# Making the second tile of weights between the second and third bank of products, with the first tile taken by two engines and the statistics taken late

## The chip, the cores and the metric

One core of a Trainium2 chip. The metric is the time of one execution on the device, in microseconds (us). The 23 runs of the kernel before on one chip lie within 0.3% of their median (4170.98 to 4191.01 us, median 4181.48). The kernel before takes 4181 us (median of 4 runs, 4176.17 to 4183.92).

## The reference, cut to what matters

Two layers. Each normalises x by groups, makes a convolution's weights for every batch element and position from a small network of z, multiplies, and adds the result to x. All is fp32.

```python
h = jax.nn.relu(_ln(z @ W1 + b1, g1, be1))
w = (h @ W2 + b2).reshape(B, L, CI, CO, K)      # weights of its own for each (b, l)
...
x_uf = jnp.stack([xp[..., i:i + L] for i in range(K)], axis=-1)
out = jnp.einsum('sbilk,bliok->sbol', x_uf, w)
out = out + bias[None]
# layer n: x = x + conv(_gn(x), ...), S2 = B = 32, CI = CO = 64, L = 256, K = 3
```

## The kernel before

The main loop runs over half batch elements `v` (64 per layer, 128 in all); one turn is called a period here. In each period TensorE makes 12 tiles of the next weights, k0 to k11 (`make`, 32 pairs of load and matmul each, 4 KiB of PSUM per partition, as much as two banks of products), and multiplies the present weights with x (`products`, four banks of PSUM, 80 pairs each). VectorE and ScalarE move the tiles into `wall`, the present weights (`take`); VectorE adds a bank of products to x (`room`) and takes the statistics for the next layer (`bn_stats`, layer 0 only). A tile may be moved into `wall` only when all products of the weights there are done. There are three buffers for tiles and two for products.

```python
ps_g = ctx.enter_context(tc.tile_pool(name="ps_g", bufs=3, space=PSUM))   # tiles of weights
ps_c = ctx.enter_context(tc.tile_pool(name="ps_c", bufs=2, space=PSUM))   # banks of products
...
def make(h, kind, o0):
    pg = ps_g.tile([P, OG, M], FP, tag="pg", name="pg")
    ...
    for k in range(OG):
        nc.tensor.matmul(pg[0:C, k, :], ...)      # line 459
        nc.tensor.matmul(pg[C:P, k, :], ...)      # line 460

def take(pg, n, kind, o0, scalar=False):
    ...
    if kind < 2:                       # all 128 partitions by VectorE
        (add_scalar if scalar else add)(slice(0, P), CH + (1 + kind) * CH)
    else:                              # lower half VectorE, upper half 8 instructions of ScalarE
        (add_scalar if scalar else add)(slice(0, C), CH + F)
        add_scalar(slice(C, P), 0)

def products(v):
    for q in range(NB):                # NB = 4
        pc = ps_c.tile([P, EB, CH], FP, tag="pc", name="pc")
        ... 80 pairs, line 505
        nc.vector.tensor_tensor(part, pc..., part, ALU.add)          # line 515
        if u < B:
            for g in range(2 * q, 2 * q + 2):
                bn_stats(parts[:, g, u, h, :], y, g)                 # line 246

order = [(kind, o) for o in starts for kind in (2, 0, 1)]
...
for v in range(1, NH * U):
    for k in range(len(order)):
        weights(v, k, False, (lambda: products(v - 1)) if k == 0 else None)   # make k0, products, take k0
        if k == 0:
            after(v - 1)               # stores, loads, next normalisation
```

## Time and profile before

| | before |
|---|---|
| time, median of 4 | 4180.99 us |
| span of the profiled run | 4177.9 us |
| period in layer 0, mean of 59 | 30.74 us |
| period in layer 1, mean of 60 | 28.91 us |
| nothing but TensorE's work (12 tiles, 4 banks, 2 changes of tile size) | 28.3 us |

The last row is the smallest period of the trace. TensorE is the bound (94% busy, and 84% of the chain that ended last), so only what makes it stand counts. "Holes" are its standing inside the products for no recorded cause; "the wait before k3" is its standing for a PSUM buffer after the products. Times of one place in all periods (the holes by their place, a tile's 32 pairs) were read off the start times of TensorE's weight loads in the trace, counted from the first product of the period. The prediction's 30.88 stands beside 30.74 here: it is met as the mean of 62 periods with the second of the loop (33.1 us) and the first two at the border between the layers (39.0 and 28.9) in it, which the table leaves out. From here on I use the table's choice for every kernel alike.

### The profile page before, as it was taken

How to read it: one execution, taken by the hardware profiler on the slowest of the kernel's cores; microseconds unless marked ns; L12 is line 12 of the kernel's file. 1: busy time of each engine (PE TensorE's matmuls, PEld its weight loads, DVE VectorE, ACT ScalarE, POOL GpSimd, SP SyncE). 2: the span in 40 equal slices, each digit the busy share in tenths (PEclk: the TensorE clock that was granted, in tenths of full speed). 3: DMA queues.
4: the chain of work that ended last, by engine and by line, in shares of the span. 5: the costliest groups of instructions: out<-in, count | busy, mean ns of one | idle time of the engine just before them, and what ended most of it. 6: DMA issues, size and time to landing. Idle time of an engine off the chain costs nothing.

```text
span 4177.9 us, 193861 instructions
## 1 busy us (share of the span) xinstructions
PE 3923.3 (94%) x90704; PEld 3746.7 (90%) x90704; DVE 2622.5 (63%) x2926; ACT 1325.8 (32%) x4384; POOL 2038.6 (49%) x628
## 2 busy tenths in 40 slices
PE   5777999999999999999998899999999999999999
PEld 3447999999999999899998899999999999999998
DVE  5686666666666666666666565655656556566565
ACT  3462322323323233232332333333323333333332
POOL 3435445445545544544551644555445554455542
PEclk8679999999999999999999999999999999999999
DMA  7875776767767677677776544544445444445442
GB/s 288 313 289 144 187 175 175 178 165 182 178 172 187 161 185 176 168 184 166 182 178 173 180 156 135 166 148 145 156 136 166 149 144 156 147 155 161 132 151 89
DMA packets 655581, 718.50 MB, mean 172 GB/s; under 512 B 568564, under 2 KB 585016, under 8 KB 586296
## 3 DMA queue, kind: packets, MB, share of 16 engines
q1 hardware_dynamic: 627796, 692.41, 58.5%
q8 instruction: 709, 11.62, 1.2%
q10 hardware_dynamic: 26980, 13.69, 1.1%
q14 instruction: 96, 0.79, 0.1%
HBM read 492.08 MB, written 213.91 MB: 169 GB/s over the span
## 4 chain that ended last, share of the span: by engine, by line
PE 84%; DVE 6%; issue 3%; DMA 2%; POOL 2%; ACT 1%; ACTq 0%; POOLq 0%; DVEq 0%; SPq 0%
PE pg L459 54%; PE pc L505 24%; PE pg L460 5%; DVE wall L471 3%; POOL xn L201 2%; DVE parts L246 1%; DVE room L515 1%; DMA hd<-xn 1%; ACT xn L218 1%; DMA zt<-in_L_conv_z_dram 1%; ACT xn L193 1%; POOL xn L446 1%; PE p L190 0%; DMA wc<-in_L_conv_Wb_dram 0%; DVE xn L446 0%
## 5 line engine op out<-in xcount | busy, mean ns | idle before, releaser
L459 PE MATMUL pg<-hT,w2t 128*64 128x128 f32 x24576 | 2733.6, 273 | 23.2 <-DVE wall L471 14.0
L460 PE MATMUL pg<-hT,w2t 128*64 128x128 f32 x24576 | 2734.3, 273 | 1.7 <-issue 1.6
L459 PEld LDWEIGHTS pg<-hT,w2t 128*64 128x64 f32 x24576 | 2683.3, 137 | 48.4 <-DVE wall L471 29.0
L460 PEld LDWEIGHTS pg<-hT,w2t 128*64 128x64 f32 x24576 | 2682.5, 137 | 3.4 <-issue 3.1
L471 DVE TENSOR_TENSOR wall<-pg,b 64x1024 f32<-64x1024 f32 x1527 | 1854.3, 1220 | 679.2 <-PE pg L460 675.2
L482 ACT ACTIVATE wall<-pg,b 64x128 f32<-64x128 f32 x4168 | 1203.8, 484 | 2662.4 <-DVE wall L471 2030.5
L436 POOL TENSOR_TENSOR xn<-room,gmean 128x2048 f32<-128x2048 f32 x124 | 581.8, 4692 | 1751.5 <-PE pc L505 1719.2
L505 PE MATMUL pc<-wall,xn 128*32 128x128 f32 (+2 forms) x40960 | 994.5, 253 | 133.3 <-issue 107.6
L505 PEld LDWEIGHTS pc<-wall,xn 128*32 128x32 f32 x40960 | 938.0, 111 | 196.7 <-issue 170.9
L515 DVE TENSOR_TENSOR room<-pc,room 128x512 f32<-128x512 f32 x512 | 354.3, 692 | 753.4 <-PE pc L505 676.6
L436 POOL TENSOR_TENSOR xn<-xn,rstd 128x2048 f32<-128x2048 f32 x124 | 746.8, 6022 | 9.7
L409 POOL TENSOR_TENSOR room<-room,bt 128x2048 f32<-128x2048 f32 x128 | 592.1, 4626 | 119.1 <-DMA bt<-bd 119.1
L246 DVE BATCH_NORM_STATS2 parts<-room 128x6 f32<-128x256 f32 (+1 forms) x592 | 241.6, 454 | 8.7
L201 POOL TENSOR_TENSOR xn<-xn 128x512 f32<-128x512 f32 (+2 forms) x192 | 104.1, 542 | 154.3 <-ACT xn L193 141.7
L190 PE MATMUL p<-wc,zt 17*128 17x256 f32 x256 | 88.4, 500 | 28.9 <-DMA zt<-in_L_conv_z_dram 28.9
L216 PEld LDWEIGHTS p<-ident,xn 128*128 128x128 f32 x256 | 50.0, 223 | 63.4 <-issue 63.4
L190 PEld LDWEIGHTS p<-wc,zt 17*128 17x128 f32 x256 | 60.8, 250 | 49.5 <-issue 27.9
L246 DVE BATCH_NORM_STATS2 parts<-wall 128x6 f32<-128x512 f32 x160 | 97.3, 677 | 7.8 <-DMA beb<-in_L_conv_beb_dram 7.8
L228 PE MATMUL p<-xn,Wb 128*64 128x512 f32 x64 | 55.2, 960 | 31.2 <-ACT xn L218 31.2
L216 PE MATMUL p<-ident,xn 128*128 128x128 f32 x256 | 61.9, 422 | 18.2 <-DVE xn L207 18.2
L205 DVE RECIPROCAL var<-var 128x8 f32<-128x8 f32 x32 | 6.4, 201 | 71.3 <-ACT var L202 71.3
L228 PEld LDWEIGHTS p<-xn,Wb 128*64 128x64 f32 x64 | 7.6, 169 | 47.2 <-ACT xn L218 44.6
(58 smaller groups left out, 266.7 us busy)
## 6 DMA issues: line engine op xcount, KB each, us to landing
bt<-bd SPq DMA_DIRECT2D x512, 256.0 KB, 5.9
room<-in_xp_dram SPq DMA_DIRECT2D x64, 1024.0 KB, 9.2
room<-in_xs_dram SPq DMA_DIRECT2D x64, 1024.0 KB, 8.2
x<-room SPq DMA_DIRECT2D x64, 1024.0 KB, 5.3
x1p<-room SPq DMA_DIRECT2D x512, 128.0 KB, 6.9
room<-x1p SPq DMA_DIRECT2D x64, 1024.0 KB, 7.9
room<-x SPq DMA_DIRECT2D x64, 1024.0 KB, 8.3
out_dram<-room SPq DMA_DIRECT2D x64, 1024.0 KB, 4.8
```

Of the source, the lines that this page charges most:

```text
L190: nc.tensor.matmul(self.p1[:, k], self.zt[:, k * P : (k + 1) * P], self.t["wc"], start=True, stop=True)
L201: nc.gpsimd.tensor_tensor(to, self.sq[:, :, 0:w], self.sq[:, :, w : 2 * w], ALU.add)
L216: nc.tensor.transpose(p2[:, net, k * P : (k + 1) * P], hs[:, 2 * k + net, :], ident)
L246: nc.vector.bn_stats(out, y.rearrange("p o (a m) -> p o a m", a=2)[:, :, :, g * e : (g + 1) * e])
L409: nc.gpsimd.tensor_tensor(y, y, bts.pop(v), ALU.add)
L436: nc.gpsimd.tensor_tensor(o, i, b, op)
L459: nc.tensor.matmul(pg[0:C, k, :], w[:, k0 * C : (k0 + 1) * C], h0, start=True, stop=True)
L460: nc.tensor.matmul(pg[C:P, k, :], w[:, k1 * C : (k1 + 1) * C], h1, start=True, stop=True)
L471: nc.vector.tensor_tensor(place(rows, a), pg[rows].rearrange("p o (t m) -> p t m o", t=NT), b2[n][rows, kind, None, None, o0 : o0 + OG].to ...
L482: nc.scalar.activation(place(rows, a)[:, :, :, k], pg[rows, k].rearrange("p (t m) -> p t m", t=NT), AF.Identity, bias=b2[n][rows, kind, o0 ...
L505: nc.tensor.matmul(pc[t * S : (t + 1) * S, n0 - q * EB : n1 - q * EB, :], xn[:, u % 2, t * MT + p + 1, :], wall[:, t, a : a + (n1 - n0) * CH],
L515: nc.vector.tensor_tensor(part, pc.rearrange("p (m a) o -> p o a m", a=2), part, ALU.add)
```

## The change

The intent: give TensorE a tile of weights to make amid the products, end the wait for the first tile sooner by sharing it between two engines, and keep the statistics out of the way of it. The core of the diff:

```diff
-        def take(pg, n, kind, o0, scalar=False):
+        def take(pg, n, kind, o0, scalar=0):
+            vector = OG - scalar          # columns 0..vector-1 VectorE, the rest ScalarE
...
-        order = [(kind, o) for o in starts for kind in (2, 0, 1)]
+        order = [(kind, o) for o in starts for kind in (0, 2, 1)]
...
-        products(NH * U - 1) and bn_stats inside products
+        products(v, banks), statistics(v, banks)
...
+        first, second = range(0, NB // 2), range(NB // 2, NB)
         for v in range(1, NH * U):
-            for k in range(len(order)):
-                weights(v, k, False, (lambda: products(v - 1)) if k == 0 else None)
-                if k == 0:
-                    after(v - 1)
+            pg0 = made(v, 0)
+            products(v - 1, first)
+            statistics(v - 1, first)
+            pg1 = made(v, 1)
+            products(v - 1, second)
+            taken(v, 0, pg0, OG // 2)     # k0: four columns VectorE, four ScalarE
+            statistics(v - 1, second)
+            after(v - 1)
+            taken(v, 1, pg1)
+            for k in range(2, len(order)):
+                weights(v, k)
```

(The two lines on `products` and `statistics` stand for a longer piece of the diff; nothing else is in it but names.)

More of the change, by code (lines that the diff above doesn't have):

```diff
@@ L468, in place, with add_vector @@
                 return at(wall[rows, 0, a : a + 1], [[WT, NT], [F, MT], [1, OG]])
-            def add(rows, a):
+            def add_vector(rows, a):
                 nc.vector.tensor_tensor(
-                    place(rows, a),
-                    pg[rows].rearrange("p o (t m) -> p t m o", t=NT),
-                    b2[n][rows, kind, None, None, o0 : o0 + OG].to_broadcast(
-                        [rows.stop - rows.start, NT, MT, OG]
+                    place(rows, a)[:, :, :, 0:vector],
+                    pg[rows, 0:vector].rearrange("p o (t m) -> p t m o", t=NT),
+                    b2[n][rows, kind, None, None, o0 : o0 + vector].to_broadcast(
+                        [rows.stop - rows.start, NT, MT, vector]
                     ),
@@ L478, in add, with add_scalar @@
                 )
-            def add_scalar(rows, a):
-                for k in range(OG):
+            def add_scalar(rows, a, k0):
+                for k in range(k0, OG):
                     nc.scalar.activation(
@@ L487, in add_scalar, with add, products @@
                     )
+            def add(rows, a):
+                if vector:
+                    add_vector(rows, a)
+                add_scalar(rows, a, vector)
             if kind < 2:
-                (add_scalar if scalar else add)(slice(0, P), CH + (1 + kind) * CH)
+                add(slice(0, P), CH + (1 + kind) * CH)
             else:
-                (add_scalar if scalar else add)(slice(0, C), CH + F)
-                add_scalar(slice(C, P), 0)
-        def products(v):
+                add(slice(0, C), CH + F)
+                add_scalar(slice(C, P), 0, 0)
+        def products(v, banks):
             u, h = divmod(v, NH)
             y = residual(v)
-            for q in range(NB):
+            for q in banks:
                 pc = ps_c.tile([P, EB, CH], FP, tag="pc", name="pc")
@@ L515, in products, with statistics @@
                 nc.vector.tensor_tensor(part, pc.rearrange("p (m a) o -> p o a m", a=2), part, ALU.add)
-                if u < B:
-                    for g in range(2 * q, 2 * q + 2):
-                        bn_stats(parts[:, g, u, h, :], y, g)
+        def statistics(v, banks):
+            u, h = divmod(v, NH)
+            if u < B:
+                for g in range(2 * banks.start, 2 * banks.stop):
+                    bn_stats(parts[:, g, u, h, :], residual(v), g)
         def next_pairs(w, k):
@@ L560, in conv_layers, with made, taken @@
         starts = range(0, CH, OG)
-        order = [(kind, o) for o in starts for kind in (2, 0, 1)]
-        def weights(v, k, scalar=False, between=None):
+        order = [(kind, o) for o in starts for kind in (0, 2, 1)]
+        def made(v, k):
+            u, h = divmod(v, NH)
+            kind, o = order[k]
+            return make(hs[u], kind, h * CH + o)
+        def taken(v, k, pg, scalar=0):
             u, h = divmod(v, NH)
@@ L567, in weights @@
             o0 = h * CH + o
-            pg = make(hs[u], kind, o0)
-            if between:
-                between()
             take(pg, n, kind, o0, scalar)
@@ L573, in weights @@
                 load_w2(n + 1, o0, o0 + OG)
+        def weights(v, k, scalar=0):
+            taken(v, k, made(v, k), scalar)
         def first_weights():
@@ L579, in first_weights @@
             for k in range(9):
-                weights(0, k, True)
+                weights(0, k, OG)
         first_phase(first_weights)
@@ L605, in conv_layers @@
                     next_pairs(B + 1, 0)
-        products(NH * U - 1)
+        products(NH * U - 1, range(NB))
         after(NH * U - 1)
```

## The prediction

> **What bounds the kernel now.** I read the page first: its busy table, its chain and its costliest groups. TensorE is the bound, and nearly all of the chain that ended last is its own work.
>
> ```profile
> PE 3923.3 (94%) x90704; PEld 3746.7 (90%) x90704; DVE 2622.5 (63%) x2926; ACT 1325.8 (32%) x4384; POOL 2038.6 (49%) x628
> PE 84%; DVE 6%; issue 3%; DMA 2%; POOL 2%; ACT 1%; ACTq 0%; POOLq 0%; DVEq 0%; SPq 0%
> L471 DVE TENSOR_TENSOR wall<-pg,b 64x1024 f32<-64x1024 f32 x1527 | 1854.3, 1220 | 679.2 <-PE pg L460 675.2
> L482 ACT ACTIVATE wall<-pg,b 64x128 f32<-64x128 f32 x4168 | 1203.8, 484 | 2662.4 <-DVE wall L471 2030.5
> q8 instruction: 709, 11.62, 1.2%
> ```
>
> The main loop runs 127 times ("periods"): 12 tiles of weights (k0 to k11, 32 load-and-matmul pairs each, 1.747 us a tile when nothing waits) and four banks of products (80 pairs each, about 1.765 us a bank). Layer 0 has 62 such periods away from the border between the layers, mean 30.88 us; layer 1 has as many, mean 28.91 us. The undisturbed sum is 12 x 1.747 + 4 x 1.765 = 28.02 us, plus 0.28 us for the two changes of tile size (from 64-column to 32-column weights 0.31 us pass between two loads, every time; back again 0.15 us). So layer 0 loses about 2.5 us a period and layer 1 about 0.6. Where, the chain of waits shows for one period of layer 0, in order of time (start, us, what):
>
> ```profile
> 2036.98 3.50 PE pc L505 x145
> 2040.49 0.82 issue
> 2041.31 2.88 PE pc L505 x113
> 2044.19 0.88 issue
> 2045.07 1.37 PE pc L505 x44
> 2046.44 0.02 issue
> 2046.46 0.70 DVE room L515
> 2047.16 0.02 issue
> 2047.19 0.75 DVE parts L246 x2
> 2047.94 2.26 DVE wall L471 x2
> 2050.20 0.04 issue
> 2050.24 0.32 PE pg L459
> ```
>
> Two things are lost here. First, two holes of "issue" inside the products. Second, after the products VectorE adds the last bank, takes two statistics and two tiles before TensorE gets a free PSUM buffer: TensorE makes k1 and k2 meanwhile and then stands 0.47 us before k3. (Mean of k3's slot in layer 0: 2.22 us, not 1.75; in layer 1, without statistics, 1.75.)
>
> The timeline of the weight loads says what the holes are:
>
> ```profile
> 2041.31 2.61 PEld L505 LDWEIGHTS pc<-wall,xn 128*32 128x32 f32 x128 [1.06 <-issue]
> 2045.07 1.19 PEld L505 LDWEIGHTS pc<-wall,xn 128*32 128x32 f32 x47 [1.15 <-issue]
> ```
>
> From hole to hole there are 128 loads and 128 matmuls, 256 instructions. In the whole trace the holes in the products sit at one place of every 256 TensorE instructions, and 181,536 of these over 256 is 709, the number of packets of the instruction queue above. TensorE runs dry of instructions: a block of products alone takes 128 x 0.022 = 2.8 us, and a new block comes 3.05 us (no hole before) to 3.6 us (after a hole) later[...]. A block with a tile of weights in it lasts 4 us and never waits. Means of the holes at the block borders (position counted in loads from the first product): layer 0, even periods 0.84 (80 to 95), 1.04 (208 to 223), 0.06 (336 to 351); odd 0.21 (16 to 31), 0.87 (144 to 158), 1.05 (272 to 286). Layer 1 even 0.01 (53 to 67), 0.26 (179 to 194), 0.64 (307 to 322); odd 0.02, 0.02 and 0.28 (243 to 259).
>
> [...]The trace has ScalarE starting only when VectorE's operation on the same tile has ended (the 2030.5 us above), although they read different halves of the partitions. In the changed tile k0 VectorE reads columns 0 to 3 and ScalarE 4 to 7, 2 KiB each[...]. [...]the trace has 1220 and 692. So VectorE's half of k0 is estimated at 0.69 us, 0.62 from its start to the next start, since the trace starts the next operation about 0.08 before the end.
>
> **The change part by part, per period.**
>
> (1) A tile (k1) goes between the second and third bank. Stream now: k0, 160 product pairs, k1 (32), 160 pairs, k2 to k11. Block borders keep their places. Layer 0 even: the border at 208 to 223 now ends a block that holds k1, so its 1.04 goes to 0; the one at 336 to 351 now ends a block of pure products: 2.8 us against some 3.15, so 0.06 becomes about 0.35; the first falls from 0.84 to about 0.40 because TensorE stands before the block's products anyway (part 3). Sum 1.94 to 0.75. Odd: 0.21 goes to 0 (same reason), 0.87 stays (a block of the first two banks only), 1.05 goes to 0. Sum 2.13 to 0.87. Mean -1.22 us. Layer 1 even: 0.91 to 0.25; odd 0.30 to 0.02; mean -0.47 us. One more change of tile size there and back: +0.28 us.
>
> (2) What VectorE does after the last bank. k0 and k1 now both sit in PSUM, so after the products TensorE has one free buffer (k2), then k0's (k3); k4 needs k2's (k1 is kind 2, its ScalarE part ends later still). VectorE's line, counted from k2's first load: add starts 0.16, next start 0.73 on, half of k0 0.62, four statistics 1.34 (twice the 0.67 that two take in the timeline), k1 1.12, k2 1.21 to its end, 0.05 to TensorE: 5.23 us. TensorE needs 1.69 + 1.75 = 3.44 for k2 and k3. So it stands 1.79 us before k4, in place of 0.47 before k3: +1.3 us in layer 0. In layer 1 without statistics the add-to-take step is 0.61: 0.16 + 0.61 + 0.62 + 1.12 + 1.21 + 0.05 = 3.77, a wait of 0.33 in place of 0. The late statistics do help k0 and k3, but k4 pays for them.
>
> (3) The order of kinds goes from (2,0,1) to (0,2,1). Kind 2 is the one whose eight ScalarE instructions start only after VectorE's, and it moves from k9 to k10, one tile nearer to the products, which read its zone from the first matmul on. In the period above:
>
> ```profile
> 2033.09 2.27 ACT L482 ACTIVATE wall<-pg,b 64x128 f32<-64x128 f32 x8 [2.97 <-DVE wall L471]
> 2064.05 2.47 ACT L482 ACTIVATE wall<-pg,b 64x128 f32<-64x128 f32 x8 [2.97 <-DVE wall L471]
> ```
>
> These end at 2035.36 and 2066.52; the products start at 2036.91 and 2067.86. One tile (1.747) later plus 0.05 for the semaphore, ScalarE ends at 2037.16 and 2068.31: the products wait 0.25 and 0.45 us. Over all periods the two values alternate, mean +0.355 us.
>
> Sum, layer 0: -1.22 + 0.28 + 1.3 + 0.355 = +0.72 us; layer 1: -0.47 + 0.28 + 0.33 + 0.355 = +0.50 us. Times 62 each: +44 and +31, in all +75 us, so 4257; I say 4255 (+1.8%). Busy work of VectorE and ScalarE hardly changes (127 halves of a tile to ScalarE, about 1.4 us each, beside other work). The phase before the loop and the border between the layers stay.
>
> **The rivals.** (a) The intended gain: the tile in the middle ends the fetch holes, and ScalarE's help with late statistics ends the wait before k3. If parts 2 and 3 cost nothing, the time falls by (1.22 - 0.28 + 0.47) x 62 + (0.47 - 0.28) x 62 = 99 us, to about 4085. Against it: the order of VectorE's queue and the three buffers are fixed by the program, and 5.23 against 3.44 is not close. (b) The fetch holes only move: the blocks find their wait at other borders, and part 1 gives 0.4 us less in each period. Then about 4305, slower by 3%. For it: [...]a block of pure products still exists in most periods. (c) All fetch holes vanish: at most 0.8 us more in layer 0 and 0.15 in layer 1, about 4198. (d) ScalarE's half of k0 is ordered after VectorE's all the same: k3 waits a microsecond more, hidden behind k4's wait in layer 0, but some 0.7 us in layer 1: about 4298. Against it: ScalarE's writes of kind 2 and VectorE's of the next tile interleave in the same zone without waiting (2048.98 and 2049.17 in the trace).
>
> **Range and chances.** The waits of parts 2 and 3 rest on durations that the trace repeats within a few hundredths; the fetch term is the loose one, by about 0.4 us a period either way, some 40 us. Range 4215 to 4300. The limit of 2% slower is 4265, ten above my figure, so: faster 0.04, within 2% 0.55, slower 0.41.
>
> **What would show it.** Right: the chain shows a VectorE wait of 1.6 to 1.9 us before the fifth tile (k4) in layer 0 and 0.2 to 0.5 in layer 1, with k0, four statistics, k1, k2 ahead of it; the first products wait for ScalarE (L482's successor) 0.25 and 0.45 in turn; "issue" holes in the products fall by about half, none left at borders whose block holds the middle tile. Wrong: no wait before k4 (part 2 falls, and the time is below 4180), or "issue" before products as large as now (part 1 falls, and it is above 4300).

## The result, and the profile after

The changed kernel takes 4291.07 us (median of 4 runs, 4282.81 to 4295.07), the one before 4180.99 us. The ratio is 1.0262 (95% interval 1.0243 to 1.0280): slower by 2.6%. Ratios here are the mean time of one kernel's runs over that of the other's of the same rounds, so not quite the ratio of the medians. The range held; the class I had given the most weight (within 2%, 0.55) did not come, the next one (0.41) did.

From the page of the changed kernel: the busy table, the chain, and groups of section 5.

```profile
PE 3972.5 (93%) x90704; PEld 3746.1 (87%) x90704; DVE 2509.8 (58%) x2926; ACT 1477.1 (34%) x4892; POOL 2037.0 (47%) x628
...
PE 71%; DVE 13%; ACT 9%; issue 3%; DMA 2%; POOL 2%; ACTq 0%; SPq 0%; POOLq 0%; DVEq 0%
...
L459 PEld LDWEIGHTS pg<-hT,w2t 128*64 128x64 f32 x24576 | 2675.9, 137 | 207.6 <-ACT wall L484 152.0
...
L484 ACT ACTIVATE wall<-pg,b 64x128 f32<-64x128 f32 (+1 forms) x4676 | 1354.6, 474 | 2621.2 <-DVE wall L473 2617.4
L473 DVE TENSOR_TENSOR wall<-pg,b 128x1024 f32<-128x1024 f32 x1527 | 1771.8, 1173 | 662.5 <-PE pg L460 662.3
```

VectorE got 83 us less of this work on line 473 and ScalarE 151 more, as planned, but the chain now holds 9% of ScalarE where it held 1%, and 13% of VectorE where it held 6%. TensorE's loads of weights stand 152 us for ScalarE. In the list of TensorE's waits of the changed kernel (us in total, times, longest) that line is first, and ScalarE also holds up the products:

```profile
PEld pg L459 <- ACT wall L484: 152.0, 131, 2.5
PEld pc L512 <- issue: 73.0, 217, 3.1
...
PEld pc L512 <- ACT wall L484: 51.7, 122, 2.2
```

In the same list of the kernel before, "issue" before products was 170.9 us, and ScalarE was in neither place:

```profile
PEld pc L505 <- issue: 170.9, 325, 3.7
...
PEld pg L459 <- DVE wall L471: 29.0, 59, 4.8
```

So the holes fell by more than half, and two waits for ScalarE came. One period of layer 0 in the chain of the changed kernel (start, us, what; pieces of make left out):

```profile
2062.73 2.26 ACT wall L484 x8
2064.99 0.04 issue
2065.03 4.05 PE pc L512 x156
2069.09 0.25 PE pg L459
...
2070.98 3.77 PE pc L512 x160
2074.75 0.03 issue
2074.78 0.69 DVE room L522
2075.47 0.60 DVE wall L473
2076.07 1.31 DVE parts L246 x4
2077.38 2.26 DVE wall L473 x2
2079.63 0.04 issue
2079.68 0.32 PE pg L459
```

It reads: the products begin 0.04 us after ScalarE's eight instructions for k10 (kind 2) end; 160 pairs, a tile, 160 pairs run without a hole; then VectorE's row is exactly the one that the prediction added up (the add, half of k0, four statistics, k1 and k2), and TensorE's k4 waits for its end. What the chain skips is k3, which had waited as well. ScalarE's timeline of this period and a period of layer 1, with VectorE's of both:

```profile
2076.18 1.26 ACT L484 ACTIVATE wall<-pg,b 128x128 f32<-128x128 f32 x4 [11.20 <-DVE wall L473]
2078.59 2.29 ACT L484 ACTIVATE wall<-pg,b 64x128 f32<-64x128 f32 x8 [1.15 <-DVE wall L473]
...
3285.92 3.54 ACT L484 ACTIVATE wall<-pg,b 128x128 f32<-128x128 f32 x12 [11.36 <-DVE wall L473]
```

```profile
2074.78 0.69 DVE L522 TENSOR_TENSOR room<-pc,room 128x512 f32<-128x512 f32 x1 [1.13 <-PE pc L512]
2075.39 0.68 DVE L473 TENSOR_TENSOR wall<-pg,b 128x512 f32<-128x512 f32 x1
...
3285.13 2.94 DVE L473 TENSOR_TENSOR wall<-pg,b 128x512 f32<-128x512 f32 x3
```

The products end at 2074.75, but ScalarE starts its half of k0 (`x4`) only at 2076.18, when VectorE's half, started at 2075.39, has ended at 2076.07. The two halves run one after the other. ScalarE ends at 2077.44; k3 reuses k0's buffer and starts at 2077.49, 1.2 us after TensorE had finished k2. In layer 1 the same: VectorE's half starts at 3285.13, ScalarE at 3285.92, and TensorE's timeline has the wait for ScalarE before k3:

```profile
3280.68 3.63 PEld L512 LDWEIGHTS pc<-wall,xn 128*32 128x32 f32 x160 [0.17 <-issue]
...
3287.22 0.13 PEld L459 LDWEIGHTS pg<-hT,w2t 128*64 128x64 f32 x1 [1.15 <-ACT wall L484]
```

Where the 115 us between the two profiled spans (4293.2 and 4177.9) lie: 59 periods of layer 0 from the third on +24.6, 62 periods of layer 1 up to the last +86.1, ahead of the loop and in its first two periods +3.0, at the border between the layers +4.1, at the end -2.4. So most of the loss is in the layer that has no statistics. By cause, us per period, holes as means of even and odd periods:

| | layer 0 predicted | layer 0 measured | layer 1 predicted | layer 1 measured |
|---|---|---|---|---|
| holes in the instruction stream | -1.22 | 2.08 to 0.78: -1.30 | -0.47 | 0.61 to 0.41: -0.20 |
| one more change of tile size and back | +0.28 | +0.29 | +0.28 | +0.29 |
| waits before k3 and k4 | +1.30 | 0.39 to 1.57: +1.18 | +0.33 | 0 to 1.14: +1.14 |
| wait of the first products for ScalarE | +0.355 | gap 0.31 to 0.55: +0.24 | +0.355 | gap 0.31 to 0.53: +0.22 |
| sum | +0.72 | +0.41 | +0.50 | +1.45 |
| period itself | | 30.74 to 31.16: +0.42 | | 28.91 to 30.32: +1.41 |

The waits are a tile's 32 pairs less what they take undisturbed: 2.89 less 1.69 for the slot that ends at k3's first load (1.20), 2.18 less 1.75 for the next (0.43); in the kernel before 2.20 less 1.75 (0.45). The tile after a wait takes 1.69 and not 1.75, so 0.06 of every such stand comes back, and the table has what is left. The change of tile size was read where no hole falls: 0.14 on the last bank and 0.15 on the tile.

### The profile page after: what moved, and what is told of

Read it like the earlier page. It is cut to its first block, busy times and chain, and to the rows that moved or that the text cites.

```text
span 4293.2 us, 194554 instructions
## 1 busy us (share of the span) xinstructions
PE 3972.5 (93%) x90704; PEld 3746.1 (87%) x90704; DVE 2509.8 (58%) x2926; ACT 1477.1 (34%) x4892; POOL 2037.0 (47%) x628
## 4 chain that ended last, share of the span: by engine, by line
PE 71%; DVE 13%; ACT 9%; issue 3%; DMA 2%; POOL 2%; ACTq 0%; SPq 0%; POOLq 0%; DVEq 0%
PE pg L459 43%; PE pc L512 23%; DVE wall L473 9%; ACT wall L484 8%; PE pg L460 3%; DVE parts L246 2%; DVE room L522 1%; POOL xn L201 1%; DMA zt<-in_L_conv_z_dram 1%; PE p L190 1%; DMA bd<-xn 1%; POOL xn L446 0%; ACT xn L218 0%; PE p L228 0%; PE p L216 0%
## 5 line engine op out<-in xcount | busy, mean ns | idle before, releaser
L459 PE MATMUL pg<-hT,w2t 128*64 128x128 f32 x24576 | 2787.8, 274 | 146.9 <-ACT wall L484 120.4
L460 PE MATMUL pg<-hT,w2t 128*64 128x128 f32 x24576 | 2787.9, 274 | 2.3 <-issue 2.1
L484 ACT ACTIVATE wall<-pg,b 64x128 f32<-64x128 f32 (+1 forms) x4676 | 1354.6, 474 | 2621.2 <-DVE wall L473 2617.4
L473 DVE TENSOR_TENSOR wall<-pg,b 128x1024 f32<-128x1024 f32 x1527 | 1771.8, 1173 | 662.5 <-PE pg L460 662.3
L409 POOL TENSOR_TENSOR room<-room,bt 128x2048 f32<-128x2048 f32 x128 | 601.0, 4696 | 124.2 <-DMA bt<-bd 104.9
L246 DVE BATCH_NORM_STATS2 parts<-room 128x6 f32<-128x256 f32 (+1 forms) x592 | 227.4, 447 | 0.0
```

Source lines behind the costliest of these rows:

```text
L246: nc.vector.bn_stats(out, y.rearrange("p o (a m) -> p o a m", a=2)[:, :, :, g * e : (g + 1) * e])
L409: nc.gpsimd.tensor_tensor(y, y, bts.pop(v), ALU.add)
L459: nc.tensor.matmul(pg[0:C, k, :], w[:, k0 * C : (k0 + 1) * C], h0, start=True, stop=True)
L460: nc.tensor.matmul(pg[C:P, k, :], w[:, k1 * C : (k1 + 1) * C], h1, start=True, stop=True)
L473: nc.vector.tensor_tensor(place(rows, a)[:, :, :, 0:vector], pg[rows, 0:vector].rearrange("p o (t m) -> p t m o", t=NT), b2[n][rows, kind, ...
L484: nc.scalar.activation(place(rows, a)[:, :, :, k], pg[rows, k].rearrange("p (t m) -> p t m", t=NT), AF.Identity, bias=b2[n][rows, kind, o0 ...
```

## The experiments

Theory A was the table: what the middle tile saves in holes it costs in buffers, and the order of kinds and the order of ScalarE after VectorE add their waits. The rivals were that the middle tile is the gain and something else the loss; that the halves of k0 are ordered by their target in SBUF and not by their PSUM tile; that the holes belong to a place in the program. Four kernels ran beside the kernel before on one chip (its median there 4181.48 us of 23 runs), then four on another (4170.11 us of 9 runs). All eight gave right results. Expected times were reckoned from 4181 us, so a run on the second chip is compared by its ratio.

**Without the middle tile.** The rest of the change stays.

```diff
             statistics(v - 1, first)
-            pg1 = made(v, 1)
             products(v - 1, second)
...
-            taken(v, 1, pg1)
+            weights(v, 1)
```

> The changed kernel without the tile between the second and third bank (k1 is made after all four banks); the rest of the change stays. Theory A (the waits for PSUM buffers after the products are what the middle tile costs, the fetch holes what it saves): layer 0 gets about 1.0 us of fetch holes back per period, loses the second change of tile size (-0.28) and nearly all of the 1.63 us that TensorE stands before k3 and k4, since k1 and k2 are made meanwhile; net about -0.9 us. Layer 1: -0.28, holes +0.1, wait before k3 1.2 to 0; net -1.4. In all some -140 us against the changed kernel, about 4150, so a little faster than before. Rival B (the middle tile brings the gain and the rest of the change the loss): slower than the changed kernel, above 4300.

Measured: 4184.51 us (20 runs), ratio to before 1.0006 (0.9996 to 1.0016). So 107 us less than the changed kernel, not 140. In layer 0 the period falls by 0.77 us: holes 0.78 to 1.87, no wait before k3 or k4 at all (each slot 1.75 or a hole). In layer 1 it falls by 0.93 where I expected 1.4: the wait before k3 is gone (-1.20), but the holes go from 0.41 to 0.85. TensorE's waits of this kernel say the same: no wait for a buffer is left among the long ones, ScalarE still holds up the products, and "issue" is back at 136.9 us, where the kernel before had 170.9:

```profile
PEld pc L512 <- issue: 136.9, 180, 2.6
...
PEld pc L512 <- ACT wall L484: 52.8, 126, 2.2
```

The middle tile is the loss and rival B falls. It pays in holes, but in its present form it costs more in buffers.

**Kind 2 back at k9.**

```diff
-order = [(kind, o) for o in starts for kind in (0, 2, 1)]
+order = [(kind, o) for o in starts for kind in ((0, 2, 1) if o < CH - OG else (2, 0, 1))]
```

> The changed kernel with the old order of kinds in the last three tiles only, so that the kind with ScalarE's eight late instructions is k9 and not k10. Theory A: the gap ahead of the first products falls from 0.55 to 0.31 us in every period, and nothing waits for ScalarE there; layer 0 gives some 0.1 of it back in fetch holes. In all -10 to -30 us, about 4270. Rival: the gap has another cause (the wait for the last tile's VectorE half) and stays, 4290.

Measured: 4275.94 us (4 runs), ratio 1.0227 (1.0209 to 1.0245), 15 us under the changed kernel. The gap ahead of the products is 0.31 us again in both layers, and the wait of products for ScalarE has left the list while the wait of k3 for ScalarE stands as it was:

```profile
PEld pg L459 <- ACT wall L484: 153.1, 133, 2.5
PEld pc L512 <- issue: 100.4, 337, 2.6
```

The 0.24 and 0.22 us of the table are shown. In layer 0 a third comes back (the period falls by 0.16), since TensorE reaches the border of the next block earlier and the holes go from 0.78 to 0.86. The growth of "issue" from 73.0 to 100.4 is mostly a change of label: with ScalarE gone as the cause, the 0.17 us that every change of tile size leaves ahead of the products is put down to "issue", 127 times.

**Two PSUM tiles for kind 0.** ScalarE's half of k0 gets a tile of its own, one bank; kinds 1 and 2 share two buffers in place of three for all. The other tiles of kind 0 are then taken by two VectorE instructions.

```diff
-ps_g = ... tile_pool(name="ps_g", bufs=3, space=PSUM)
+ps_g = ... tile_pool(name="ps_g", bufs=2, space=PSUM)
+ps_h = ... tile_pool(name="ps_h", bufs=1, space=PSUM)
...
+            if kind == 0:       # columns 0-3 in one tile, 4-7 in the other
+                pair = [ps_h.tile([P, OG // 2, M], FP, tag=t, name=t) for t in ("pa", "pb")]
```

> The changed kernel with each tile of kind 0 in two PSUM tiles of one bank each, so that ScalarE's half of k0 has a tile of its own; the other kinds share two buffers. Theory A (ScalarE's half of k0 starts after VectorE's because the two read one tile, and this makes k3 wait): ScalarE starts with VectorE, the wait before k3 goes from 1.2 us to 0; in layer 1 a wait of 0.3 before k4 stays, net -0.9 us per period; in layer 0 the wait moves to k4 (1.6 us in all as now), net 0. In all -50 us, about 4240, less what the phase before the loop loses with two buffers (0 to 10 us). Rival (they are ordered because they write one zone of the weights' tile in SBUF): no change, 4290.

Measured: 4337.75 us (4 runs), ratio 1.0374 (1.0357 to 1.0392). As a time this missed by far, and the trace says where: the loop's first products start at 413.0 us against 328.5, so the phase ahead of the loop, which uses the same buffers for other things, lost 85 us with two of them, not 10. The loop itself did what theory A says. ScalarE's and then VectorE's timeline of one period of layer 0:

```profile
2118.38 1.26 ACT L504 ACTIVATE wall<-pb,b 128x128 f32<-128x128 f32 x4 [10.21 <-PE pc L532]
```

```profile
2118.44 0.69 DVE L542 TENSOR_TENSOR room<-pc,room 128x512 f32<-128x512 f32 x1 [1.13 <-PE pc L532]
2119.05 0.68 DVE L493 TENSOR_TENSOR wall<-pa,b 128x512 f32<-128x512 f32 x1
```

ScalarE starts when the products end, 0.67 us before VectorE's half, and what ended its idle time is TensorE. The writes to the target still interleave as before, so the rival falls: what ordered them was the shared PSUM tile. The slot before k3 is 1.69 in both layers, no wait. In layer 1, k4 waits 0.33 us, the figure that the prediction had added up for it, and the period is 29.21, down 1.11 from the changed kernel. In layer 0, k4 waits 1.62, and the period is 31.56, up 0.40, because the holes are 1.16 where they were 0.78.

**The kernel before with the block borders moved.** Two tiles are made in vain ahead of the first weights.

```diff
+            for k in range(2):
+                make(hs[0], 0, 0)
             for k in range(9):
                 weights(0, k, True)
```

> The kernel before with two tiles made in vain ahead of the first weights: 64 loads and 64 matmuls, 128 instructions, so that every border of 256 TensorE instructions moves by 64 loads against the program. Theory A (the holes in the products are waits for the next block of instructions): in layer 0 the even periods get the holes of the odd ones and the other way: even near 16-31, 144-158, 272-286 loads after the first product, odd near 80-95, 208-223. The time stays within 0.5%. Rival (the holes belong to a place in the program, a transfer or a buffer): even periods keep theirs near 80-95 and 208-223.

Measured: 4141.39 us (4 runs), ratio 0.9905 (0.9884 to 0.9926). The holes moved as theory A says: in layer 0 those of even periods fall at 144 to 159 and 272 to 287 loads after the first product, of odd ones at 208 to 222. The weight loads of one and the same even period of layer 0 (the products of v = 54), in the kernel before and then in the shifted one:

```profile
2005.74 1.90 PEld L505 LDWEIGHTS pc<-wall,xn 128*32 128x32 f32 x82 [0.17 <-issue]
2008.32 2.96 PEld L505 LDWEIGHTS pc<-wall,xn 128*32 128x32 f32 x128 [0.68 <-issue]
2012.34 2.52 PEld L505 LDWEIGHTS pc<-wall,xn 128*32 128x32 f32 x110 [1.06 <-issue]
```

```profile
1950.75 3.44 PEld L505 LDWEIGHTS pc<-wall,xn 128*32 128x32 f32 x146 [0.17 <-issue]
1954.75 2.71 PEld L505 LDWEIGHTS pc<-wall,xn 128*32 128x32 f32 x128 [0.56 <-issue]
1958.77 1.19 PEld L505 LDWEIGHTS pc<-wall,xn 128*32 128x32 f32 x46 [1.30 <-issue]
```

The count before the first hole goes from 82 to 146, by the 64 loads added, and from hole to hole there are 128 in both. The rival falls. What I had not expected is the gain: the period of layer 0 fell by 1.09 us and that of layer 1 rose by 0.49. The holes of odd periods in layer 0 nearly vanished (2.13 to 0.29 us), those of even ones fell from 2.03 to 1.60. So how large a hole is depends on the period it falls in as well as on the block.

The kept traces say what a hole waits for. Their DMA packets include those of the instruction queue (q8), 709 or 710 of 16 KiB each. In the main loops of the ten kernels 1325 gaps of more than 0.3 us lie between two loads of products. Ten are at the border between the layers, one in each kernel. The other 1315 all stand at one count of TensorE's instructions (193 or 194 of every 256, with the semaphore instructions of its queue counted in), and each ends 1.18 to 1.69 us (median 1.41) after the end of a q8 packet. So the holes are waits for the next block. In the kernel before, such a packet took 1.05 us (median), and blocks of products alone took about 3.1 us from border to border where the first border had no hole and 3.75 us where it had one (medians), against the 2.8 us of their pairs. A load of data transfers at the time is not needed for a large one. In the period of v = 53 of the kernel before, gaps of 1.00 and 1.14 us end at 1979.21 and 1982.95, while the 16 DMA engines were 2% busy. The stretch from 1978 to 1983 us reads (busy us of PE, PEld, DVE, ACT and POOL, then the clock, the DMA share and GB/s):

```profile
1978.00:1983.00 5.00, 3.39 (x152) 3.08 (x144) 3.41 (x8) 0.00 (x0) 0.00 (x0) 1.00 0.02 4
```

Holes come in chains: between two borders with products alone, the packet started 1.29 us after the first border where that had a hole and 0.54 where it had none, and the second border's hole was 1.01 and 0.42 us (medians of the holes over 0.1 us, kernel before).

**k0 by VectorE alone.**

```diff
-            taken(v, 0, pg0, OG // 2)
+            taken(v, 0, pg0, 0)
```

> The changed kernel with k0 taken by VectorE alone, no ScalarE half. Theory A (ScalarE's half runs after VectorE's, so the split saves VectorE 0.5 us and delays k0's buffer): in layer 0 the waits before k3 and k4 become 0.45 and 1.84 us, 2.3 in all against 1.63; in layer 1 0.33 and 0.5, 0.83 against 1.2. So layer 0 slower by 0.66 and layer 1 faster by 0.37 per period, about 4309 in all, with some 20 us either way from where the block borders fall. Rival (the split is a gain in both layers, as meant): slower in both, above 4340.

Measured: 4309.36 us (4 runs), ratio 1.0339 (1.0322 to 1.0356). TensorE's timeline of a period in layer 1, two waits for VectorE, before k3 and before k4:

```profile
3296.38 0.13 PEld L459 LDWEIGHTS pg<-hT,w2t 128*64 128x64 f32 x1 [0.32 <-DVE wall L473]
...
3298.64 0.13 PEld L459 LDWEIGHTS pg<-hT,w2t 128*64 128x64 f32 x1 [0.53 <-DVE wall L473]
```

The mean waits are 0.33 and 1.81 in layer 0, 0.34 and 0.50 in layer 1, close to what was expected. The split of k0 is worth 0.78 us of each period in layer 0 and costs 0.65 in layer 1 (29.66 without it, 30.32 with it). Only 0.36 of that 0.65 is the waits (1.20 against 0.84); the rest, less 0.05 the other way in the gap ahead of the products, is holes: 0.41 us in the changed kernel, 0.08 here. The reason shows in the semaphore instructions of TensorE before the loads of tiles; the view of that line, in the kernel before and in the changed one:

```profile
L459 PEldq EVENT_SEMAPHORE  x79: 51/51/51, 278.3 to 4102.8; - x79
```

```profile
L459 PEldq EVENT_SEMAPHORE  x202: 51/51/746, 278.7 to 4260.7; - x101
```

The changed kernel has 123 more, about one a period: k3's first load waits for two engines and takes one instruction more to do so. The instruction itself is short (51 ns, median), but it moves the borders of the blocks by one instruction a period. In layer 1 they lie at other places than before, and there some blocks hold products alone in spite of the middle tile. With k0 taken by one engine the borders are where they were before (81 to 95 and 54 to 68 loads into even periods), and the middle tile leaves next to no hole in layer 1, as in the run with two tiles.

**Late statistics alone on the kernel before.**

```diff
-                if u < B:
-                    for g in range(2 * q, 2 * q + 2):
-                        bn_stats(parts[:, g, u, h, :], y, g)
+                if q < NB // 2:
+                    statistics(v, q)       # banks 0 and 1 as before
...
+                if k == (0 if soon else 1): # banks 2 and 3 after k1 is taken
+                    for q in range(NB // 2, NB):
+                        statistics(v - 1, q)
```

(`soon` is true in two periods whose statistics are needed at once.)

> The kernel before with one part of the change alone: the statistics of the third and fourth bank are taken after k0 and k1 have left PSUM. Theory A: the wait of 0.47 us before k3 in layer 0 goes, layer 1 is as before: -29 us, about 4152. Rival (the wait comes back at another tile, as it did in the changed kernel): 4181.

Measured: 4156.76 us (6 runs), ratio 0.9971 (0.9960 to 0.9983), that is some 12 us off and not 29. The slot before k3 is 1.75 in layer 0, so the wait of 0.47 is gone and didn't come back at another tile. But the period of layer 0 is 0.29 under that of the kernel before, not 0.47: the wait had cost 0.39, since the tile after it had been 0.06 quicker, and the four banks take 0.07 longer, with holes of 2.15 for 2.08. Layer 1, where the edit changes nothing, is 0.09 shorter here too (28.82 and 28.91), so traces of different sessions can differ by about 0.1 us a period. With that taken off, 0.2 us in 62 periods is the 12 us.

**The change without the middle tile and with kind 2 at k9.** Both edits above.

> The changed kernel without the middle tile and with kind 2 back at k9, so what is left of the change is the split of k0, the late statistics and the order of kinds elsewhere. Theory A: the 0.23 us ahead of the products go in every period against the run without the middle tile, less what comes back as fetch holes: about 4158. Rival: as without the middle tile, 4184.

Measured: 4146.64 us (4 runs), ratio 0.9944 (0.9926 to 0.9961). The gap ahead of the products is 0.31 us, no tile waits, and the periods are 30.21 and 28.96. So what is left of the change is a small gain of 0.6%.

**Late statistics with the borders placed.** Two tiles in vain ahead of the first weights and two at the border between the layers, so that layer 0 has the shifted borders and layer 1 its old ones.

```diff
+            for k in range(2):
+                make(hs[0], 0, 0)
             for k in range(9):
                 weights(0, k, True)
...
+                    for j in range(2):
+                        make(hs[B], 0, 0)
                     spread()
```

> Late statistics alone on the kernel before, with two tiles made in vain ahead of the first weights and two more at the border between the layers: the block borders move by 64 loads in layer 0 and are back at their old places in layer 1. Theory A (holes belong to block borders, and their size to the load of the transfers in that period): layer 0 has the small holes of the shifted run and no wait before k3, some 29.2 us per period; layer 1 as in the kernel before, 28.9. About 4090. Rival (the gain of the shifted run was chance): as late statistics alone.

Measured: 4102.45 us (4 runs), ratio 0.9845 (0.9830 to 0.9859): faster than both kernels, by 1.55% than the one before. Periods 29.64 and 28.77. The first is above the 29.2 expected: the holes of odd periods in layer 0 came to 1.0 us where the shifted run had 0.29. That their size follows the load of the transfers is not borne out at the border where most of it lies (208 to 222 loads): in the 4 us before the hole's end the DMA engines were 24% busy in the shifted run and 30% here. The packet with the next block started 0.74 us after the border before in that run and 1.28 here; from its start to the end of the hole it was 2.45 and 2.48. What makes it start later stays open. The chain that ended last is TensorE's for 90%, 84% in the kernel before:

```profile
PE 90%; POOL 2%; issue 2%; DMA 2%; ACT 2%; DVE 1%; ACTq 0%; POOLq 0%; DVEq 0%
```

## Why the prediction was right or wrong

The time held: +75 us forecast, +110 measured by the medians. But the two layers are wrong in opposite ways, and part of the agreement is luck: +44 forecast for layer 0 and some +26 measured (0.42 x 62), +31 for layer 1 and +86 measured.

- Part 1, the holes. In layer 0 the working holds within 0.08 us: -1.22 and -1.30. The borders at 208 to 223 and 272 to 286 lost their holes (1.04 to 0.09, 1.05 to 0.01), the block of pure products at 336 to 351 gained one (0.06 to 0.37, forecast 0.35), the block of the first two banks kept most of its own (0.87 to 0.70). In layer 1 the step that failed is "Block borders keep their places". They didn't: one more semaphore instruction a period moved them, and -0.47 became -0.20. The runs that keep the places (k0 by VectorE alone, two tiles) have next to no holes in layer 1. In layer 0 they moved too, by some 30 loads more than before over the layer: in even periods the one at 190 fell to 161 and then into the middle tile, which follows load 160. None passed it, so each block kept its kind; that the sum holds there owes something to luck. The prediction's rule that a block with a tile of weights in it never waits is contradicted by its own list: the border at 80 to 95, with a hole of 0.84, ends a block that holds k0 and lasts 4.26 us.
- Part 2, VectorE's row. The durations are those of the trace: in the kernel before, VectorE's instruction of 1024 elements took 1220 ns (line 471, mean) and that of 512 took 692 (line 515); half of k0, 512 elements, took 680 in the changed kernel (line 473, mean of 127). The order is in the trace, and where nothing else interferes the sum is met: k4 waits 0.33 us in layer 1 with two tiles (forecast 0.33), 1.62 in layer 0 (forecast 1.79). One term was too large there: from the add to k0 it is 0.61 us (2074.78 to 2075.39 above), as the prediction has it for layer 1, and not 0.73, the step from an add to the statistics in the kernel before. That is 0.12 of the 0.17. But in the changed kernel another wait comes first. The step that failed is the one that let the halves of k0 run together; that was shown by no trace of the kernel before. The argument against rival (d) rested on the target in SBUF, and that part was right, but the order comes from the PSUM tile that both read: with one tile ScalarE started 0.11 us after VectorE's end (2076.18 and 2076.07), with a tile for each 0.67 us ahead of VectorE's start. Rival (d) is what happened in this point: it had +0.7 us in layer 1 and 4298, and it measured +0.87 (1.20 for 0.33) and 4291.
- Part 3, the order of kinds. The mechanism is shown, by the wait in the changed kernel's list (51.7 us, 122 times) and by the run that undoes it (the gap is 0.31 us again). Its size was off: the term "0.25 and 0.45 in turn" came from ScalarE's group of 2.27 and 2.47 us in turn, and in the changed kernel the group takes 2.25 in every period. It measured 0.24 and 0.22.
- The intended gain, rival (a): the holes do fall and the statistics do leave k0's way, but without the middle tile the same change costs nothing and with it 107 us. Rival (c) is out: the holes did not vanish. Rival (b), that they only move, fails in layer 0, but in layer 1 it is in part what happened: the borders moved, and part 1 gave 0.27 us less than forecast (it had 0.4).

What stays open is why the packet with the next block starts at so different times after the border before, and with it why a hole at the same place has so different a size in even and odd periods and from run to run (0.29 and 1.0 us with the same borders).

## What to carry to other kernels

Before a tile is made earlier, count the buffers it holds: from the moment that the consumers are blocked, the producer has only the free buffers, and the wait comes back at the first tile that needs one, here k4 in place of k3 (in layer 0, 1.62 us before k4 in the run with two tiles, against 0.45 before k3 in the kernel before). Two engines that read one PSUM tile may run one after the other although they read different columns of it: here ScalarE's half of k0 waited for VectorE's and started 0.11 us after its end, and with a tile for each it started 0.67 us ahead of VectorE's. So look in the trace whether they overlap, or give each a tile. A stream of many short TensorE instructions can be bound by the fetch of instructions, as the products here (0.022 us a pair, holes of 2.08 us a period in layer 0 of the kernel before); then one instruction more a period matters: here it cost 0.33 us of holes in layer 1, nearly as much as the change of the waits themselves (0.36). So look where the block borders lie before two variants are compared: moving them by 64 loads took 0.95% off the time of the kernel before.
